# Transfers spaced by matmul work, and the fourth expert pass sent home by scatters: a macaron layer with experts

## The chip, the cores and the metric

The kernel runs on one core of one Trainium2 chip. The metric is the device time of one execution in microseconds (us), lower is better; the value quoted is the median of three runs. The core's engines are TensorE (PE, with its weight loads PEld), VectorE (DVE), ScalarE (ACT), GpSimd (POOL) and SyncE (SP). POOL issues the indirect DMAs, SP the plain ones.

## The reference

Eight sequences of 512 tokens with 128 features (D) pass through a feed-forward layer with experts, an attention, and the same feed-forward layer again, each on a layernorm of its input with a residual. All in float32.

```python
x = x + 0.5 * ffn(layernorm(x))
x = x + attn(layernorm(x))
x = x + 0.5 * ffn(layernorm(x))

def ffn(x):          # 8 experts, each token goes to its best 2
    logits = x @ router_w + router_b
    scores, idx = top_k(logits, 2); gates = softmax(scores)
    for each expert e:   # c_e: the token's gate for e, or 0
        out += (relu(x @ W1[e] + b1[e]) @ W2[e] + b2[e]) * c_e    # 128 -> 512 -> 128

def attn(x):         # 16 heads of 8, causal, over each sequence
    q, k, v = x @ w_qkv;  q, k rotated in half of the heads
    p = softmax(q k^T / sqrt(8) + decay bias, causal)
    return (p v) @ w_o
```

## The kernel before

**Six expert passes.** Only the two experts of each token are computed. For this the tokens are sorted by expert: each normalised token row is scattered twice into a "room" in DRAM (`xs`), which has a fixed number of rows for each expert (351 or 480). An expert pass then runs over the eight experts of a room: it fetches an expert's rows by a plain DMA (`xb`, L933), transposes them (`turn`, L976), multiplies by W1 in pieces of 128 hidden features (`wide`, L989, with the relu on ACT, L996), and by W2 in tiles of up to 120 rows (`out`, L1013, with the bias on DVE, L1017, into `ysb`). The first feed-forward layer has the passes f0 (sequences 0 and 1, 351 rows), f1 (2, 3, 4; 480) and f2 (5, 6, 7; 480), the second g0, g1 and g2 over the same sequences.

**Routing.** `route` does for one sequence: layernorm (statistics L758 and L761, variance L763 on DVE, `rstd` on POOL by a power, recorded at L474, `xn` L769 on DVE), transposes on PE (L784) and their copy on DVE (L786), router logits (L814, L818), ranks and places (L827 to L870, `posb` at L857, `to` at L866), and eight scatters of 128 rows on POOL (L875). The attention of a sequence has a layernorm of the same form (`rstd_a`, `xn_a`).

**Two ways back to the tokens.** f0, f1, f2 and g0 are untagged: SP writes an expert's results to DRAM (`ys`, 175.5 or 240 KB) by one plain DMA (L1024), and POOL later gathers them by token, eight gathers of 128 rows a sequence (`combine`, recorded at L474), each pair followed by two DVE additions with the gates (L1073). g1 and g2 are tagged: a token row carries its home address in two more columns; `homes` (three small DVE operations an expert, L943 to L951) turns it into row numbers, POOL scatters each result tile to its token's place (`send`, L957), and `collect` (L1110) reads a sequence back by plain loads into `yr` and adds on DVE (L1114).

**The order.** The work is laid out in units: a lead (units -30 to -1: f0 and most of f1's start), a core (0 to 95: eight sequences, four head groups and three steps each, of the attention, with the rest of f1, then f2, g0 and the start of g1 between them) and a tail (96 to 126: g1's rest and g2). `surround` emits one unit: a quota of pieces of the running expert pass, the unit's attention work, and the due steps of other streams (`at`, `routed`, `combined`, each given a unit). PE, ACT, DVE and SP follow an order written by hand from that; on POOL `in_turn` keeps the program's order. Indirect DMAs are queued as jobs (scatters and gathers) or results (sends), and `transfer()` records the next one:

```python
    def transfer(self, second=False):

        if self.jobs and (
            not second or any(urgent for urgent, _ in self.jobs)
            or (len(self.jobs) > 4 and not self.results)
        ):
            self.jobs.popleft()[1]()
        elif self.results:
            self.results.popleft()()
```

A unit calls it after the first causal mask, at its end, and in the tail also once between. Each recorded transfer waits for the evacuation of a matmul result that was the newest when it was recorded (its "mark", `behind_mark`). Spare DMAs on SP clear the rooms ahead of their use; those of rooms 3 and 4 wait in `later`, one for each unit from unit 12 on.

Of the kernel before, what the change touches and what calls it, by code (L numbers as in the profile page):

```python
# [11 lines left out]
FP = mybir.dt.float32  # L12
# [8 lines left out]
P = 128  # L21
B, N, D = 8, 512, 128
T = N // P
# [22 lines left out]

ROOMS = [(2, 351, False), (3, 480, False), (3, 480, False), (3, 480, True), (3, 480, True)]
CAP = max(cap for _, cap, _ in ROOMS)  # L50
NOWHERE = 1e6
CT = -(-CAP // P)
STOP = object()

# [394 lines left out]
class Group:  # L449


    def __init__(self, seqs, cap, key, xs, ys, tagged):
        self.seqs, self.cap, self.key, self.xs, self.ys = seqs, cap, key, xs, ys
        self.tagged, self.width = tagged, D + 2 * tagged
        self.ct = -(-cap // P)
        self.rows = cap // self.ct
        assert self.ct * self.rows == cap
        self.parts = [(t, min(3 if cap > 4 * P else 4, self.ct - t))
                      for t in range(0, self.ct, 3 if cap > 4 * P else 4)]
        self.placed = 0  # L460
        self.pieces = E * (len(self.parts) * (1 + C) + self.ct) + 1


# [19 lines left out]
class Main:  # L483
    def __init__(self, tc, ctx, aps):
# [15 lines left out]


        self.jobs, self.results, self.mark = deque(), deque(), None
        self.adds, self.unit = deque(), 0
        const = self.const

# [48 lines left out]
            partial(nc.sync.dma_start, self.wo_sb, aps["w_o"]),  # L554
        ])
        self.loads.extend(partial(self.clear, 2, t) for t in range(4))
        self.later = deque(partial(self.clear, i, t) for i in (3, 4) for t in range(4))
        self.later.extend(partial(self.clear_results, i) for i in (3, 4))


        self.ident = ident = const.tile([P, P], FP, name="ident")
# [88 lines left out]
# [6 lines that stand above are left out]
            self.jobs.popleft()[1]()  # L656
        elif self.results:
            self.results.popleft()()

    def additions(self):  # L660

# [262 lines left out]
    def experts(self, g):  # L924
# [31 lines left out]
        def send(e, t, ys):  # L956
            ins = nc.gpsimd.indirect_dma_start(  # L957
                out=g.ys[:, :],
                out_offset=bass.IndirectOffsetOnAxis(ap=home[e][:rows, t : t + 1], axis=0),
                in_=ys[:rows, t, :], in_offset=None,  # L960
            ).ins
            tc.declare_no_dep(ins, group=f"ys_{key}", reason="no two rows have the same home")
            tc.add_to_no_dep_group(f"ys_{key}", ins)
            self.in_turn(ins, scatter=True)
            self.behind_mark(ins)

        def up(e, xb):

            xT = self.fp.tile([P, CAP], FP, tag="xT", name=f"xT_{key}_{e}")
            h = self.fp.tile([P, C, CAP], FP, tag="h", name=f"h_{key}_{e}")  # L970

            def turn(t0, nt):
                n0, n = t0 * rows, nt * rows
                tp = self.bank([P, N], f"xbT_ps_{key}_{e}_{t0}")
                for t in range(nt):
                    nc.tensor.transpose(  # L976
                        tp[:, ts(t, rows)], xb[:rows, t0 + t, :D], self.ident[:rows, :rows]
                    )
                if self.evac == "act":
                    nc.scalar.copy(xT[:, n0 : n0 + n], tp[:, :n])  # L980
                else:
                    nc.vector.tensor_copy(xT[:, n0 : n0 + n], tp[:, :n])
                if g.tagged and t0 == 0:
                    homes(e, xb)

            def wide(t0, nt, c):
                n0, n = t0 * rows, nt * rows
                z = self.bank([P, N], f"z_{key}_{e}_{n0}_{c}")
                nc.tensor.matmul(  # L989
                    z[:, :n], self.w1_sb[:, e, ts(c, P)], xT[:, n0 : n0 + n],  # L990
                    start=True, stop=True,
                )
                bias = self.b1T[:, e * C + c : e * C + c + 1]
                dst = h[:, c, n0 : n0 + n]
                if self.evac == "act":
                    ins = nc.scalar.activation(dst, z[:, :n], AF.Relu, bias=bias)  # L996
                else:
                    ins = nc.vector.tensor_scalar(dst, z[:, :n], bias, 0.0, ALU.add, ALU.max)  # L998
                self.mark = ins.ins

            return (
                h, [partial(turn, *p) for p in g.parts],
                [partial(wide, *p, c) for p in g.parts for c in range(C)],
            )

        def down(e, h):

            ys = self.fp.tile([P, CT, D], FP, tag="ysb", bufs=5, name=f"ysb_{key}_{e}")

            def out(t):  # L1010
                y = self.bank([P, D], f"y_{key}_{e}_{t}")
                for c in range(C):
                    nc.tensor.matmul(  # L1013
                        y[:rows], h[:, c, ts(t, rows)], self.w2_sb[:, e, c, :],
                        start=(c == 0), stop=(c == C - 1),
                    )
                ins = nc.vector.tensor_tensor(  # L1017
                    ys[:rows, t, :], y[:rows], self.b2_sb[:rows, e], ALU.add
                )
                self.mark = ins.ins  # L1020
                if g.tagged:
                    self.results.append(partial(send, e, t, ys))
                elif t == g.ct - 1:
                    nc.sync.dma_start(  # L1024
                        g.ys[: E * g.cap, :].rearrange("(t p e) d -> e p t d", p=rows, e=E)[e],
                        ys[:rows, : g.ct],
                    )

            return [partial(out, t) for t in range(g.ct)]
# [69 lines left out]
    def collect(self, g, i, dst, parts=1):  # L1099

        nc = self.nc
        b = g.seqs[i]
        x = self.x[b]
        if i % 2 == 0:
            self.pair = self.p2.tile([P, 2, T, 2, D], FP, tag="ee", name=f"yr_{b}")
        yr = self.pair[:, i % 2]
        src = g.ys[2 * N * i : 2 * N * (i + 1), :].rearrange("(t p r) d -> p t r d", p=P, r=2)
        n = T // parts
        for k in range(parts):
            nc.sync.dma_start(yr[:, ts(k, n)], src[:, ts(k, n)])  # L1110
        yield
        for t in range(T):
            for r in range(2):
                nc.vector.scalar_tensor_tensor(  # L1114
                    x[:, t, :], yr[:, t, r], g.gates[:, i, t, r : r + 1], x[:, t, :],
                    ALU.mult, ALU.add,
                )
            if t % n == n - 1:
                k = t // n
                nc.sync.dma_start(  # L1120
                    dst[b].rearrange("(t p) d -> p t d", p=P)[:, ts(k, n)], x[:, ts(k, n)]
                )
            if parts == 1:
                yield
# [179 lines left out]
def macaron_kernel(  # L1304
# [24 lines left out]
    def run(*streams):  # L1329
        for s in streams:  # L1330
            for _ in s:
                pass
# [23 lines left out]
    with ExitStack() as main:  # L1356
# [5 lines left out]
        f0 = m.open_group([0, 1], 351, 0, "f0")  # L1362
        f1 = m.open_group([2, 3, 4], 480, 1, "f1")
        f2 = m.open_group([5, 6, 7], 480, 2, "f2")
        g0 = m.open_group([0, 1], 351, 1, "g0")
        g1 = m.open_group([2, 3, 4], 480, 3, "g1")
        g2 = m.open_group([5, 6, 7], 480, 4, "g2")
        order = [f0, f1, f2, g0, g1, g2]
# [55 lines left out]
        ]  # L1424
        fills = {}

        def surround(n, att):

            m.unit = n
# [21 lines left out]
                    m.oT = (*m.held[:2], got)  # L1451
            m.held = (*units[n], ee) if att else None
            m.evac = "dve" if att and n % seq not in (8, 9, 10) else "act"
            run(take(fill, 1 if quota else 0))
            m.evac = "act"
            if att:
                m.causal(units[n][2], ee, 0)
            m.transfer()
            if last is not None:
                m.outputs(*last)  # L1460
            if att:
# [5 lines left out]
            for k, (stream, steps) in enumerate(work):  # L1467
                some = todo // (len(work) - k + 1)
                run(take(stream, steps))
                run(take(fill, some))  # L1470
                todo -= some
            if n >= core and len(m.jobs) + len(m.results) > 2:
                run(take(fill, todo // 2))
                todo -= todo // 2
                m.transfer(second=True)
            run(take(fill, todo))
            m.additions()
            m.transfer(second=True)

        m.held = m.oT = None  # L1480
        with m.banks(("m", 8)):
# [22 lines left out]
            for b in range(B):  # L1504
                u = b * seq
                if b == 2:
                    combined(7, f1, 0, urgent=True, ahead=True)
                elif b > 2:
                    combined(u - (17 if b == 5 else 21), *place[True][b], urgent=b == 5, ahead=b == 5)
                if b > 0:  # L1510
                    at(u - 10, m.project(b), 8)
                for g in range(G):
# [1 line left out]
                at(u + seq + 2, m.finish(b), 2, 2 if b == B - 1 else 1)  # L1514
                routed(u + seq + (3 if b == B - 1 else 4), *place[False][b], urgent=b in (1, 4, 5, 6, 7), ahead=b in (4, 6, 7))
            for i in range(2):
                combined(79 + 7 * i, g0, i, out)
            for i in range(3):
                at(tail + 2 + 3 * i, m.collect(g1, i, out), 5)
            at(tail, m.verdict(bad), 2)  # L1520
# [76 lines left out]
```

## Time and profile before

| | before |
|---|---|
| three runs, us | 700.78, 701.87, 702.69 |
| median, us | 701.87 |
| the profiled execution, us | 700.09 |
| its span, us | 698.3 |
| mean granted PE clock | 0.977 |
| PE busy | 629.2 us, 90% |
| DVE busy | 410.2 us, 59% |
| ACT busy | 341.3 us, 49% |
| POOL busy | 300.3 us, 43%, 322 instructions |
| scatters into rooms, L875 | first layer 40 at 974 ns and 24 at 989 ns, second layer 64 at 998 ns |
| gathers, recorded at L474 | first layer 64 at 1013 ns, second layer 16 at 1053 ns |
| sends, L957 | 64, 996 ns each |

A profile is one execution; its span runs from the first to the last instruction, and the execution's own time is 1.8 us longer. Rows of a timeline give the start, the duration, engine, line and operation, then output and inputs by the names in the program without their numbers, and in brackets how long the engine stood idle before and what released it. `xn_f` is thus the `xn` of any sequence of the first layer, `xn_g` of the second, `xn_a` of the attention. In the clock row of the slices a 9 is full speed.

### The profile page before, as it was taken

The page shows a single profiled execution, that of the slowest core. Times are in us where ns is not written, and L with a number is a line of the kernel's source. Part 1 is how long each engine was busy: PE and PEld are TensorE (multiplying, and loading weights), DVE is VectorE, ACT ScalarE, POOL GpSimd, SP SyncE. Part 2 cuts the span into 40 slices and gives each one's busy share as a digit, 9 for nine tenths or more (in the row PEclk, how much of TensorE's full clock was granted, in tenths as well). Part 3 has the DMA queues.
Part 4 walks back from the last instruction along what each step waited for, and adds up shares of the span by engine and source line. Part 5 has one row for each costly group of instructions (what it writes and reads, how often), then busy time and mean ns, then how long its engine had stood idle before and what let it go on. Part 6 is the DMA issues. An engine that isn't in the chain of part 4 may idle for free. (4 is left out here: it accounts for less than half of the span.)

```text
span 698.3 us, 13045 instructions
## 1 busy us (share of the span) xinstructions
PE 629.2 (90%) x4867; PEld 410.3 (59%) x4867; DVE 410.2 (59%) x1442; ACT 341.3 (49%) x548; POOL 300.3 (43%) x322
## 2 busy tenths in 40 slices
PE   3269999999999999999999999999999998969980
PEld 2148867756465656556656656656456656747760
DVE  6736448734466666675687677676666654433414
ACT  4034443455755656565665565555665552234420
POOL 3744637642223223314154423424144556575660
PEclk9999999999999999999999999999999999889995
DMA  8747843312409921111211111101402111145324
GB/s 265 197 136 209 205 115 98 85 45 77 101 22 172 264 69 38 30 29 43 71 32 49 40 38 38 30 27 39 105 27 75 35 31 42 53 121 140 104 58 143
DMA packets 78670, 61.06 MB, mean 87 GB/s; under 512 B 7392, under 2 KB 70792, under 8 KB 78600
## 3 DMA queue, kind: packets, MB, share of 16 engines
q1 hardware_dynamic: 69608, 42.51, 23.8%
q0 software_dynamic: 8704, 17.63, 8.5%
q8 instruction: 41, 0.67, 0.4%
q14 instruction: 29, 0.24, 0.1%
q10 hardware_dynamic: 288, 0.01, 0.0%
HBM read 26.34 MB, written 33.78 MB: 86 GB/s over the span
## 5 line engine op out<-in xcount | busy, mean ns | idle before, releaser
L1208 ACT ACTIVATE ee<-st 128x768 f32<-128x768 f32 (+1 forms) x192 | 159.0, 881 | 104.1 <-PE st L1201 100.6
L474 POOL DMA_INDIRECT yt_f<-ys,back_f x64 | 64.8, 1013 | 133.5 <-DVE ee L1215 55.7
L1215 DVE TENSOR_TENSOR ee<-ee,keep 128x256 f32<-128x256 f32 (+1 forms) x192 | 93.5, 507 | 25.4 <-ACT ee L1208 25.3
L1013 PEld LDWEIGHTS y_g<-w_sb,h_g 128*120 128x120 f32 (+1 forms) x704 | 87.1, 184 | 27.4 <-issue 21.7
L875 POOL DMA_INDIRECT xs<-xn_g,to_g x64 | 63.8, 998 | 90.1 <-DVE ee L1215 34.9
L1013 PEld LDWEIGHTS y_f<-w_sb,h_f 128*120 128x120 f32 (+1 forms) x704 | 85.9, 182 | 28.5 <-issue 16.2
L1201 PE MATMUL st<-qT,kT 32*128 32x512 f32 (+3 forms) x1024 | 96.1, 467 | 2.3 <-ACT h_f L996 0.8
L1013 PE MATMUL y_f<-w_sb,h_f 128*120 128x128 f32 (+1 forms) x704 | 93.9, 277 | 0.2 <-DVE h_f L998 0.2
L989 PE MATMUL z_g<-xT_g,w_sb 128*128 128x480 f32 (+1 forms) x192 | 92.6, 569 | 1.3 <-ACT xT_g L980 1.3
L1013 PE MATMUL y_g<-w_sb,h_g 128*120 128x128 f32 (+1 forms) x704 | 93.0, 277 | 0.6 <-DVE o_tok L1250 0.3
L1227 PE MATMUL o<-ee,vpad 128*32 128x512 f32 (+3 forms) x1024 | 89.4, 442 | 0.8 <-DVE ee L1215 0.8
L989 PE MATMUL z_f<-xT_f,w_sb 128*128 128x480 f32 (+1 forms) x192 | 88.8, 551 | 1.0 <-ACT xT_f L980 1.0
L996 ACT ACTIVATE h_f<-z_f,b1T 128x480 f32<-128x480 f32 (+1 forms) x86 | 53.5, 623 | 68.2 <-PE z_f L989 67.3
L957 POOL DMA_INDIRECT ys<-ysb_g,home_g x64 | 63.7, 996 | 39.3 <-ACT h_g L996 8.7
L1017 DVE TENSOR_TENSOR ysb_f<-y_f,b_sb 120x128 f32<-120x128 f32 (+1 forms) x88 | 25.0, 287 | 77.9 <-PE y_f L1013 74.2
L996 ACT ACTIVATE h_g<-z_g,b1T 128x480 f32<-128x480 f32 (+1 forms) x71 | 45.7, 646 | 47.4 <-PE z_g L989 46.7
L1201 PEld LDWEIGHTS st<-qT,kT 32*128 32x128 f32 x1024 | 43.1, 183 | 32.6 <-issue 8.1
L1017 DVE TENSOR_TENSOR ysb_g<-y_g,b_sb 120x128 f32<-120x128 f32 (+1 forms) x88 | 25.1, 287 | 58.2 <-PE y_g L1013 57.6
L1227 PEld LDWEIGHTS o<-ee,vpad 128*32 128x32 f32 x1024 | 23.5, 108 | 52.4 <-issue 7.5
L875 POOL DMA_INDIRECT xs<-xn_n,to_f x40 | 39.0, 974 | 34.9 <-ACT xi_sb L727 8.1
L989 PEld LDWEIGHTS z_g<-xT_g,w_sb 128*128 128x128 f32 x192 | 30.1, 195 | 26.6 <-issue 15.2
L989 PEld LDWEIGHTS z_f<-xT_f,w_sb 128*128 128x128 f32 x192 | 30.2, 194 | 13.8 <-issue 7.2
(186 smaller groups left out, 778.7 us busy)
## 6 DMA issues: line engine op xcount, KB each, us to landing
w_sb<-in_L_ffn_W_dram SPq DMA_DIRECT2D x16, 256.0 KB
xs<-zeros SPq DMA_DIRECT2D x8, 487.5 KB
xb_g<-xs SPq DMA_DIRECT2D x16, 243.8 KB
xb_f<-xs SPq DMA_DIRECT2D x16, 240.0 KB
ys<-ysb_f SPq DMA_DIRECT2D x16, 240.0 KB
ys<-zeros SPq DMA_DIRECT2D x2, 1536.0 KB
x<-in_L_attn_x_dram SPq DMA_DIRECT2D x8, 256.0 KB
xs<-zeros SPq DMA_DIRECT2D x1, 1920.0 KB
```

The source lines that it names most:

```text
L474: ins = op(*args, **kw)
L875: ins = nc.gpsimd.indirect_dma_start(out=g.xs[:, :], out_offset=bass.IndirectOffsetOnAxis(ap=g.to[:, i, t, r : r + 1], axis=0), in_=xn[:, ...
L957: ins = nc.gpsimd.indirect_dma_start(out=g.ys[:, :], out_offset=bass.IndirectOffsetOnAxis(ap=home[e][:rows, t : t + 1], axis=0), in_=ys[:r ...
L989: nc.tensor.matmul(z[:, :n], self.w1_sb[:, e, ts(c, P)], xT[:, n0 : n0 + n], start=True, stop=True,)
L996: ins = nc.scalar.activation(dst, z[:, :n], AF.Relu, bias=bias)
L1013: nc.tensor.matmul(y[:rows], h[:, c, ts(t, rows)], self.w2_sb[:, e, c, :], start=(c == 0), stop=(c == C - 1),)
L1017: ins = nc.vector.tensor_tensor(ys[:rows, t, :], y[:rows], self.b2_sb[:rows, e], ALU.add)
L1201: nc.tensor.matmul(st[:, h, c0 : c0 + N - kt * P], kT[r0 : r0 + SLOT, ts(kt, P)], qT[r0 : r0 + SLOT, kt * P :], start=True, stop=True,)
L1208: nc.scalar.activation(ee[:, two, :width], st[:, two, :width], AF.Exp)
L1215: ins = self.nc.vector.tensor_tensor(d, d, self.keep.unsqueeze(1).unsqueeze(1).to_broadcast([P, 2, len(parts), P]), ALU.min,)
L1227: self.nc.tensor.matmul(self.o[h * SLOT : (h + 1) * SLOT, kt * P :], self.vpads[b % 2][:, kt, 4 * g + h, :], ee[:, h, c0 : c0 + n], start= ...
```

## The change

There are two parts. First, g0 becomes a tagged pass with a room of its own (a sixth, with one more set of clears): its 24 result tiles are scattered by `send`, and `collect` reads its two sequences back in the core, at units 82 and 88. The 16 gathers of g0 and its 8 plain result writes are gone. The gathers of four sequences are entered two units earlier, and those of sequences 6 and 7 as urgent. `ysb` has four buffers for five.

Second, outside the core a unit no longer has fixed places for transfers. `work` counts the columns that PE has been given (transposed rows, the width of each wide product, 512 for a result tile, and 350 for each step of another stream); after each piece a transfer is recorded if the count is at 830 or over, and each transfer takes 830 off. In the core a unit has its two places as before.

```diff
-ROOMS = [(2, 351, False), (3, 480, False), (3, 480, False), (3, 480, True), (3, 480, True)]
+ROOMS = [(2, 351, False), (3, 480, False), (3, 480, False), (3, 480, True), (3, 480, True), (2, 351, True)]
+SPACING = 830
...
-        self.later = deque(partial(self.clear, i, t) for i in (3, 4) for t in range(4))
-        self.later.extend(partial(self.clear_results, i) for i in (3, 4))
+        self.later = deque()
+        for i, parts in ((5, 3), (3, 4), (4, 4)):
+            self.later.extend(partial(self.clear, i, t) for t in range(parts))
+            self.later.append(partial(self.clear_results, i))
...
         elif self.results:
             self.results.popleft()()
+        self.work = max(self.work - SPACING, 0)
...
+                self.work += nt * rows          # turn
...
+                self.work += n                  # wide
...
-            ys = self.fp.tile([P, CT, D], FP, tag="ysb", bufs=5, name=f"ysb_{key}_{e}")
+            ys = self.fp.tile([P, CT, D], FP, tag="ysb", bufs=4, name=f"ysb_{key}_{e}")
...
+                self.work += C * D              # out
...
-        if i % 2 == 0:
+        if self.unit < 96:
+            self.pair = self.p1.tile([P, 1, T, 2, D], FP, tag="yr", name=f"yr_{b}")
+        elif i % 2 == 0:
             self.pair = self.p2.tile([P, 2, T, 2, D], FP, tag="ee", name=f"yr_{b}")
-        yr = self.pair[:, i % 2]
+        yr = self.pair[:, i % self.pair.shape[1]]
...
-        g0 = m.open_group([0, 1], 351, 1, "g0")
+        g0 = m.open_group([0, 1], 351, 5, "g0")
...
+        def pieces(fill, n, att):
+
+            for _ in take(fill, n):
+                if not att and m.work >= SPACING:
+                    m.transfer()
+                yield
...
-            run(take(fill, 1 if quota else 0))
+            run(pieces(fill, 1 if quota else 0, att))
             m.evac = "act"
             if att:
                 m.causal(units[n][2], ee, 0)
-            m.transfer()
+                m.transfer()
...
-                run(take(fill, some))
+                run(pieces(fill, some, att))
                 todo -= some
-            if n >= core and len(m.jobs) + len(m.results) > 2:
-                run(take(fill, todo // 2))
-                todo -= todo // 2
+                if not att:
+                    m.work += 350
+            run(pieces(fill, todo, att))
+            m.additions()
+            if att:
                 m.transfer(second=True)
-            run(take(fill, todo))
-            m.additions()
-            m.transfer(second=True)
...
-                    combined(u - (17 if b == 5 else 21), *place[True][b], urgent=b == 5, ahead=b == 5)
+                    combined(u - (17 if b == 5 else 23), *place[True][b], urgent=b > 4, ahead=b == 5)
...
-                combined(79 + 7 * i, g0, i, out)
+                at(82 + 6 * i, m.collect(g0, i, out), 5)
```

More of the change, by code (lines that the diff above doesn't have):

```diff
@@ L459, in __init__ @@
                       for t in range(0, self.ct, 3 if cap > 4 * P else 4)]
-        self.placed = 0
+        self.placed = self.sent = 0
         self.pieces = E * (len(self.parts) * (1 + C) + self.ct) + 1
@@ L502, in __init__ @@
         self.jobs, self.results, self.mark = deque(), deque(), None
+        self.work = 0
         self.adds, self.unit = deque(), 0
@@ L965, in send @@
             self.behind_mark(ins)
+            g.sent += 1
         def up(e, xb):
@@ L1103, in collect @@
         x = self.x[b]
-        if i % 2 == 0:
+        if self.unit < 96:
+            self.pair = self.p1.tile([P, 1, T, 2, D], FP, tag="yr", name=f"yr_{b}")
+        elif i % 2 == 0:
             self.pair = self.p2.tile([P, 2, T, 2, D], FP, tag="ee", name=f"yr_{b}")
-        yr = self.pair[:, i % 2]
+        yr = self.pair[:, i % self.pair.shape[1]]
+        assert g.sent == E * g.ct
         src = g.ys[2 * N * i : 2 * N * (i + 1), :].rearrange("(t p r) d -> p t r d", p=P, r=2)
```

## The prediction

> **What bounds the kernel now.** The page's first two sections come first: engine shares, then slices.
>
> ```profile
> span 698.3 us, 13045 instructions
> PE 629.2 (90%) x4867; PEld 410.3 (59%) x4867; DVE 410.2 (59%) x1442; ACT 341.3 (49%) x548; POOL 300.3 (43%) x322
> PE   3269999999999999999999999999999998969980
> PEclk9999999999999999999999999999999999889995
> ```
>
> PE is 90% busy, and every slice from the fifth (70 us) to the 33rd is full. Time can be won or lost only where PE waits: in the first 45 us, which the change leaves alone, and between 580 and 620 us. What is now hidden beside a full PE can only become a loss. The windows of that stretch (columns: length, PE, PEld, DVE, ACT, POOL busy, clock, DMA share, GB/s) and PE's timeline there say what it waits for.
>
> ```profile
> 580.00:600.00 20.00, 17.25 (x93) 13.26 (x92) 9.52 (x41) 4.34 (x7) 11.97 (x12) 0.83 0.13 39
> 600.00:620.00 20.00, 14.68 (x89) 11.08 (x88) 6.53 (x29) 4.54 (x8) 13.72 (x15) 0.88 0.44 113
> ...
> 589.66 1.26 PE L784 MATMUL xnT_ps_g<-ident,xn_g 128*128 128x128 f32 x4 [1.87 <-DVE xn_g L769]
> 591.71 1.88 PE L814 MATMUL lg_ps_g<-rw_sb,xnT_g 128*128 128x8 f32 x8 [0.78 <-DVE xnT_g L786]
> ...
> 616.69 1.03 PE L976 MATMUL xbT_ps_g<-ident,xb_g 120*128 120x120 f32 x4 [4.67 <-DMA xb_g<-xs]
> ```
>
> The last sequence's layernorm (1.87 us) opens a chain, router, 8 scatters, fetch, whose end PE waits 4.67 us for. From 616.69 us on PE is full to 677 us, so a microsecond won in the chain is won at the end. POOL's timeline at its head, and in the lead, where two layernorms pass through the same queue:
>
> ```profile
> 587.15 1.00 POOL L474 DMA_INDIRECT yt_g<-ys,back_g  x1 [0.31 <-issue]
> 588.16 1.06 POOL L474 TENSOR_TENSOR rstd_g<-var_g,neg_half 128x4 f32<-128x4 f32 x1
> ...
> 82.15 0.96 POOL L875 DMA_INDIRECT xs<-xn_n,to_f  x1 [0.30 <-issue]
> 83.41 0.96 POOL L875 DMA_INDIRECT xs<-xn_n,to_f  x1 [0.30 <-issue]
> ...
> 78.28 1.07 POOL L474 TENSOR_TENSOR rstd_f<-var_f,neg_half 128x4 f32<-128x4 f32 x1
> 116.33 1.04 POOL L474 TENSOR_TENSOR rstd_f<-var_f,neg_half 128x4 f32<-128x4 f32 x1
> 117.36 1.00 POOL L474 TENSOR_TENSOR rstd_a<-var_a,neg_half 128x4 f32<-128x4 f32 x1
> ```
>
> A transfer holds POOL for 0.97 us and the next starts 0.30 us later: one per 1.27 us (82.15 to 83.41). An rstd stands in the same queue in program order, behind every transfer recorded before it; PE's transposes L784 stand behind that.
>
> **The change, part by part.** The instruction orders of both programs give PE and ACT unchanged; DVE, POOL and SP differ.
>
> *Tail.* All gathers of g0 are gone from POOL, the one at 587.15 among them. rstd then follows the send that ends at 586.85: 586.87 for 588.16, a gain of 1.3 us in the chain. Two additions L1073 (0.73 us at 598.05), which stood ahead of posb L857, go too. What is next depends on the clock. PE's clock is 0.5 from 591.24 to 598.06 us, two stretches of 3.41 us, and logits, transposes, a wide pair and eight second products take 1.88, 1.04, 1.82 and 1.92 us there for 0.96, 0.58, 0.97 and 1.04 elsewhere: 3.1 us more. With the idle 1.87 cut to about 0.6 that fall may not come. Gain: 1.3 us if it does; if not, posb moves from 598.69 to about 594.8, the scatters' first from 600.92 to 597.0, and the gain is 3.9. The wait of 4.67 us stays, since PE's work before it moves too. One scatter gap of 1.40 us among the eight may go (1.1 us more), so the ends are 1.3 and 5.0; I take 3.0, nearer to the fall staying out, because the idle is cut by two thirds.
>
> *Lead.* Spacing lets a transfer out for each 830 columns of PE work. In f1's pass PE takes 1.68 us (103.56 to 105.24) for two wide products and one result tile, 960 + 512 columns, so 830 columns are 0.95 us, less than the 1.27 us slot. POOL then runs without pause, and more transfers than before stand ahead of each rstd. By slots and before's evacuation times:
> - Before rstd of sequence 5 now stand all 16 scatters of sequences 3 and 4. They start at 61.40 (mark 61.13): 61.40 + 16 x 1.27 - 0.30 = 81.42, so rstd ends at 82.49 (79.35 before). PE's L784 began at 81.19; xn takes 1.2 us of DVE and the last transpose follows 0.4 later: end 84.12 for 81.79, a stall of 2.3. The fetch of f1, for which PE waited 0.84 us at 90.58, no longer waits for these scatters: -0.8. Net 1.5.
> - Gathers of f0 start at 94.72 (96.2 with that shift). Eight gathers and two scatters precede rstd of sequence 6: 96.2 + 10 x 1.27 - 0.3 + 1.07 = 109.7 (105.69). xn, L784 end at 111.2; before 108.3, with the shift 109.8. Stall 1.4, sum 2.9.
> - Ten more slots precede the rstds of sequence 7 and of attention 0: 109.7 + 0.19 + 12.4 = 122.3, ends 123.4 and 124.4 (117.37, 118.36). Attention's L784 then ends at 125.95; before 120.46, shifted 123.4. Stall 2.6, sum 5.5.
> - DVE keeps its order, and in the new one four additions of sequence 1 stand ahead of the copies L786 of sequence 7 (120.51 before). The last one's gather ends at 125.35 + 1.5 = 126.85. From a gather's end to its data no row of the lead is bound; a scatter's end at 87.03 released a fetch at 88.38, and the last send's end at 681.55 landed at 683.35: 1.35 to 1.8, I take 1.6. Additions and copies then give L814 its input at 130.1, where it would have begun at 128.35. Stall 1.9, sum 7.4.
> - The additions that ended at 135.83 ahead of qpad L1165 are gone, and with them PE's wait of 0.88: 6.5 us.
>
> Lower bound: if POOL's transfers come back inside the slots as PE's own lateness spreads, the last two stalls go: 1.5 + 1.4 - 0.9 = 2.0. Upper bound: each stall could halve the clock as the one at 587.80 did, 3.1 us a time: 6.5 + 6.2 for two.
>
> A rule and this row part here. In the trace PE's clock fell at 591.24 after a stretch of 3.41 us (from 587.83) with 2.2 us of idle and sparse transposes in the rest. The Trainium skill (TensorE: Matmul & The Clock Gate, Part 1 and its table of advice) has the clock halve after an idle window of about 3.4 us that runs freely, and advises against idle gaps over about 3 us; by that no lead stall costs more than its length, and by the row each may. The page adds that transposes do not count as busy in the same way, which would join the two, and 6.83 us is two of its windows. I take the middle: no fall in the likeliest case, one in the next.
>
> *Core.* 24 home operations on DVE (L943, 947, 951: 0.16, 0.17, 0.16 us at 596.11), eight trios of 0.5 us. PE's L1227 waited 0.8 us in all for DVE over 1024 matmuls, so they lie under cover; uncovered they cost 8 x 0.5 = 4.0. 24 sends for 16 gathers are 8 x 1.27 = 10 us of POOL, which is 43% busy; the order leaves each attention rstd where it stood. The plain loads of g0: one of g1 was issued at 633.06 and used at 639.06, 6.0 us; g0's first goes out at about 499.5 and is used after 514. Removed additions and added ones are both 16. Clears of 2.5 MB more ride in slices that moved 172 and 264 GB/s: some 10 us of DMA time, and f1's additions have 5.6 us of slack. Bounds -1 to +4, taken +0.5: the nearest row, PE's 0.8 us, says covered. Fewer buffers for results (4 for 5) cost nothing while a result leaves within four experts, some 50 us in the core; without that cover an expert waits one 1.27 us slot.
>
> **Sum.** +6.5 +0.5 -3.0 = +4.0. The profiled execution took 700.09 us around its span of 698.3, so 704.1; the median of the runs is 701.87, 1.8 more than that execution, so 705.9 us. A measurement here can tell 0.3%, about 2.1 us, from no change.
>
> **Rivals.**
> - *Faster.* POOL's train breaks up and only the first lead stalls are paid (+2.0), while the clock's fall in the tail stays out and the odd gap goes (-5.0), core 0: -3.0, 698.9 us. For it: the tail is worth its gain undiluted. Against: the slots of 1.27 us at 16.92 to 25.45 us show that POOL does not go faster, and the marks of the third train have passed up to 6 us before its slots come (109.95 for 116.00). It decides at the third rstd: started before about 119 us, this side wins.
> - *Nothing to measure.* +3.5 in the lead, as the third stall overlaps the fourth, +0.5, -4.0: 701.9.
> - *Slower still.* One lead stall fills a clock stretch, or two: 705.9 + 3.1 = 709.0, or 712.1. For it the row at 591.24; against it that lead stalls are interleaved with matmuls that are dense.
> - *The change does not space.* If 830 columns seldom bind, transfers leave as before in number: lead 0, tail -3.0, 698.9. The new order speaks against it: rstd stands behind more transfers, not fewer. It is part of the faster side's chance.
>
> **How the numbers follow.** The sum as worked out, 0.45; slower still, 0.17; nothing to measure, 0.20; faster, 0.18. The range reaches from the faster case's figure, 698.9, to 711.5, which leaves out the end of the two-fall case. The likeliest case's own range is 703.6 to 707.8 (tail 5.0 to 1.3, landing 1.35 to 1.8). Faster 0.18, same 0.20, slower 0.62.
>
> **What would show it.** rstd in the lead at 81.4, 108 to 109 and 122 to 124 us, ending right behind unpaused transfers, and PE's L784 waiting for xn by 1 to 3 us each. PE's attention starting 5 to 7 us later than at 136.81. In the tail, rstd right behind a send, L814 at 0.96 us instead of 1.88, and the wait for the fetch still near 4.7 us. Wrong, if the lead's L784 show no wait, if the clock row shows 0.5 in the lead, or if PE waits in the core for DVE.

## The result and the profile after

The changed kernel takes 706.43 us (median; 704.91 to 707.51), the kernel before 701.87: a ratio of 1.0066, interval 1.0052 to 1.0080, 4.6 us slower. The profiled execution took 707.51 us around its span of 705.4, the longest of its runs, while that of before (700.09) lies below all of its own, so the two traces differ by 7.1 us, more than the medians do. Of the seven runs after, the two fastest (704.91, 704.97) are the two with a granted PE clock of 0.98; the other five, the profiled one among them, have 0.975 to 0.977. Line numbers have moved: L784 is now L789, L875 is L880, L957 is L962, L976 is L982, L1073 is L1082.

Engine shares and slices of the profile after:

```profile
span 705.4 us, 13078 instructions
PE 633.4 (90%) x4867; PEld 412.1 (58%) x4867; DVE 413.6 (59%) x1470; ACT 341.8 (48%) x548; POOL 309.0 (44%) x331
PE   3269999899999999999999999999999998979970
PEclk9999999999999999999999999999999999889995
```

PE has the same 4867 instructions and one slice below 9 in what was its unbroken stretch. PE's timeline after (start, duration, and in brackets the wait and its releaser), in the lead and then in the tail:

```profile
83.34 1.01 PE L789 MATMUL xnT_ps_f<-ident,xn_f 128*128 128x128 f32 x4 [1.64 <-DVE xn_f L774]
111.31 1.25 PE L789 MATMUL xnT_ps_f<-ident,xn_f 128*128 128x128 f32 x4 [1.37 <-DVE xn_f L774]
125.40 1.10 PE L789 MATMUL xnT_ps_f<-ident,xn_f 128*128 128x128 f32 x4 [2.11 <-DVE xn_f L774]
...
596.88 1.09 PE L789 MATMUL xnT_ps_g<-ident,xn_g 128*128 128x128 f32 x4 [0.84 <-DVE xn_g L774]
598.76 1.88 PE L819 MATMUL lg_ps_g<-rw_sb,xnT_g 128*128 128x8 f32 x8 [0.78 <-DVE xnT_g L791]
622.59 1.03 PE L982 MATMUL xbT_ps_g<-ident,xb_g 120*128 120x120 f32 x4 [3.37 <-DMA xb_g<-xs]
```

Three waits for `xn` that were not there now stand in the lead. In the tail the two waits are shorter (0.84 for 1.87, 3.37 for 4.67). The logits still take 1.88 us, so PE was again at half clock. POOL's timeline shows what `xn` waits for:

```profile
79.50 0.96 POOL L880 DMA_INDIRECT xs<-xn_n,to_f  x1 [0.30 <-issue]
80.77 0.96 POOL L880 DMA_INDIRECT xs<-xn_n,to_f  x1 [0.30 <-issue]
81.75 1.06 POOL L475 TENSOR_TENSOR rstd_f<-var_f,neg_half 128x4 f32<-128x4 f32 x1
...
122.86 1.04 POOL L475 DMA_INDIRECT yt_f<-ys,back_f  x1 [0.30 <-issue]
123.92 1.05 POOL L475 TENSOR_TENSOR rstd_f<-var_f,neg_half 128x4 f32<-128x4 f32 x1
124.95 1.00 POOL L475 TENSOR_TENSOR rstd_a<-var_a,neg_half 128x4 f32<-128x4 f32 x1
```

Transfers stand back to back, 1.27 us apart, and rstd follows right behind the last of them. It starts at 81.75, 109.79, 123.92 and 124.95 us where before had 78.28, 104.64, 116.33 and 117.36.

Since PE runs the same instructions in the same order, each can be set against itself. PE stands 0.34 us behind before at 45.8 us, 2.5 after the first L789, 4.6 after the second, 6.9 to 7.3 after the third, 8.8 from 131.0 us on, 7.8 at qT (L1190, 144.57), 8.2 from 351.8 us on, 7.2 at the last layernorm, 5.9 at the fetch (622.59) and 6.6 from 629 on.

### The profile page after: what moved, and what is told of

Its sections match the earlier page's. It is cut to its first block, busy times and chain, and to the rows that moved or that the text cites. A ratio compares the mean times of both kernels' runs of the same rounds, so it can differ in the third digit from the quotient of the medians.

```text
span 705.4 us, 13078 instructions
## 1 busy us (share of the span) xinstructions
PE 633.4 (90%) x4867; PEld 412.1 (58%) x4867; DVE 413.6 (59%) x1470; ACT 341.8 (48%) x548; POOL 309.0 (44%) x331
## 5 line engine op out<-in xcount | busy, mean ns | idle before, releaser
L962 POOL DMA_INDIRECT ys<-ysb_g,home_g x88 | 88.6, 1007 | 88.9 <-DVE ysb_g L1025 21.1
L880 POOL DMA_INDIRECT xs<-xn_g,to_g x64 | 63.7, 995 | 92.9 <-DVE ee L1227 24.6
L1025 DVE TENSOR_TENSOR ysb_f<-y_f,b_sb 120x128 f32<-120x128 f32 (+1 forms) x88 | 25.0, 288 | 75.5 <-PE y_f L1021 71.9
L1025 DVE TENSOR_TENSOR ysb_g<-y_g,b_sb 120x128 f32<-120x128 f32 (+1 forms) x88 | 25.1, 288 | 62.5 <-PE y_g L1021 61.7
L880 POOL DMA_INDIRECT xs<-xn_n,to_f x40 | 38.9, 974 | 30.5 <-ACT h_f L1003 12.5
```

The source lines that it names most:

```text
L880: ins = nc.gpsimd.indirect_dma_start(out=g.xs[:, :], out_offset=bass.IndirectOffsetOnAxis(ap=g.to[:, i, t, r : r + 1], axis=0), in_=xn[:, ...
L962: ins = nc.gpsimd.indirect_dma_start(out=g.ys[:, :], out_offset=bass.IndirectOffsetOnAxis(ap=home[e][:rows, t : t + 1], axis=0), in_=ys[:r ...
L1025: ins = nc.vector.tensor_tensor(ys[:rows, t, :], y[:rows], self.b2_sb[:rows, e], ALU.add)
```

## The experiments

Ratios are to the kernel before on the same chip, with 95% intervals; a difference in us behind a ratio is worked out from the ratio, unless medians are named.

**Where the price lies.** The queue theory says that the lead's transfers ahead of rstd cost everything and the tail gains. The rival says that g0's new way home costs it. `m.spaced` switches the spacing on for some units only.

`lead_old`: the fixed places back in the lead alone.

```diff
-                if not att and m.work >= SPACING:
+                if m.spaced and m.work >= SPACING:      # m.spaced = n >= core
...
+            if not m.spaced:
+                m.transfer()                            # and second=True, as before
```

> The changed kernel with the lead's two fixed places for transfers put back; the tail stays spaced and g0 stays tagged. Queue theory (the lead's loss is rstd waiting in POOL's queue): rstd of sequences 5, 6, 7 and of attention 0 at 78.3, 104.6, 116.3 and 117.4 us as before, no wait at L789 in the lead, PE level with before until 580 us; the tail keeps its 2.3 us; about 699.6 us. Rival (the price lies in g0's scatters, homes, loads and clears in the core): 704 to 706 us, with PE falling behind between 140 and 580 us.

Measured 700.36 us against 702.66 for before on that chip, ratio 0.9966 (0.9951 to 0.9982): 2.4 us faster. No wait at L789 is left in the lead, and PE does not fall behind between 140 and 340 us. The 3.3 us that it is behind before at 134 us come from its start (0.9) and from the f1 fetch (1.24 us of wait for 0.84, and one stretch of half clock behind it, 94.44 to 97.86), not from a layernorm.

`lead_only`: the same switch as `m.spaced = n < 0`, with g0 untagged and before's units for the gathers.

> The kernel before with the spacing in the lead alone; g0 untagged, core and tail with their fixed places. Queue theory: the whole lead loss, rstd at 81.4, 108 to 111, 121 to 126 us, PE about 8 us late at 140 us, no gain in the tail: about 709.5 us. Rival (price in g0's way home): 702 us, as before.

Measured 710.54 us, ratio 1.0123 (1.0102 to 1.0144): 8.6 us slower than before (7.9 by the medians), against the rival's zero. Its waits on PE (in total, times, longest) are those of the changed kernel:

```profile
PE xnT_ps_f L789 <- DVE xn_f L774: 5.1, 3, 2.1
```

`tag_only`: `m.spaced = False`, g0 tagged.

> The changed kernel with fixed places for transfers everywhere, so that g0's scatters and plain loads (with their clears and the earlier gathers) stand alone. Queue theory: lead as before; in the tail the gather ahead of rstd and two additions ahead of posb are gone, 1.0 to 2.3 us: about 700.2 us. Rival (price in g0's way home): 704 to 706 us.

Measured 702.0 us, ratio 0.9985 (0.9971 to 0.9998): 1.1 us faster (0.7 by the medians), at or below the low end of the 1.0 to 2.3 us that were expected. With fixed places a send has taken the gather's place ahead of the last rstd: PE's wait there is 1.85 us, as before. Only the scatters' start came earlier, 12.9 us after the last variance for 14.9. So the 1.0 us by which that wait is shorter in the changed kernel belongs to the tail's spacing and not to the gather's removal alone.

**Is it rstd's place, or the spacing as such?** `hold` keeps everything and records no transfer in the units of the lead's layernorms.

```diff
+HOLD = (-22, -21, -14, -13, -10, -9)
...
-                if not att and m.work >= SPACING:
+                if not att and m.work >= SPACING and m.unit not in HOLD:
```

> The changed kernel, with one addition: in six units of the lead (the two in which each of the three layernorms there is computed) no transfer is recorded, so that POOL has drained when rstd comes; the spacing is the same otherwise. Queue theory: rstd at 78.0, 104.6, 116.3 and 117.4 us, no waits at L789 in the lead, the old waits of 0.84 us (fetch of f1) and 0.88 us (qpad) smaller, tail gain 2.3 us: about 698.5 us. Rival (spacing costs by crowding the DMA queues or DVE, wherever rstd stands): PE still 4 to 8 us late at 140 us, about 705 us.

Measured 699.28 us, ratio 0.9954 (0.9937 to 0.9971). One line takes the lead's whole loss away: PE stands 0.5 to 1.5 us behind before up to 140 us, 1.1 of it from before the first layernorm. rstd waits for its variance again, not for the queue:

```profile
105.66 1.04 POOL L476 TENSOR_TENSOR rstd_f<-var_f,neg_half 128x4 f32<-128x4 f32 x1 [3.87 <-DVE var_f L769]
117.58 1.05 POOL L476 TENSOR_TENSOR rstd_f<-var_f,neg_half 128x4 f32<-128x4 f32 x1 [3.09 <-DVE var_f L769]
```

The f1 fetch (0.81 us) and qpad (1.02) still wait, which the expectation had put lower. `hold_again`, on a third chip:

> The kernel hold once more, as the base for the three beside it: about 0.995 of the kernel before. Rival (its lead over before belongs to one chip): 1.00 or above.

699.48 against 702.78 us, ratio 0.9947 (0.9926 to 0.9968).

**The size of the spacing, and the clock, on a chip apart.** Four kernels ran on a second chip, where the kernel before takes 715.71 us.

`lead_1000` takes 1000 columns for 830 where the unit is below 0.

> The changed kernel with 1000 columns for 830 in the lead alone. Queue theory, by slots of 1.27 us and the marks of before: rstd of sequences 5, 6, 7 and attention 0 at 78.9, 104.9, 117.5 and 118.6 us, at most 1.2 us later than before, so waits at L789 of 1 us or less in all; about 700 us. Rival (spacing by matmul work costs whatever its size, by crowding DMA queues or DVE): PE 4 to 8 us late at 140 us, about 705 us.

Ratio 1.0084 (1.0055 to 1.0113). The time is inconclusive: PE waits there 4.12 us at L1214 for an `h_f` (from 154.56) and 3.34 us at L850 (from 141.13); in the traces from the other chips these two products wait 0.75 us at most. The three kernels below ran on the same chip with the lead of `hold`, and they wait at the same two products, 3.3 to 4.4 us and 1.7 us. So these waits go with the chip and not with the 1000 columns; what makes them stays open. Neither the changed kernel nor `hold` ran on that chip. Its trace does bear on the queue: L790 waits 0.9 us in all in the lead, for 5.1 at 830 columns, though PE's own lateness there gives POOL some of that time.

The other three add matmuls that nothing reads, to `hold`; `warm_all`, and `warm_all2` further on, also record no transfer in unit 100, between the last rstd and the last scatters:

```diff
+    def warm(self, n, key):
+        z = self.bank([P, N], f"warm_{key}")
+        for _ in range(n):
+            self.nc.tensor.matmul(
+                z[:, :480], self.ident, self.w1_sb[:, 0, :480], start=True, stop=True)
...
+        if key == "g2_7": self.warm(2, "a")       # ahead of the transposes, and "b" ahead of the logits
...
+        if key == "g2": self.warm(7, "c")         # in experts, ahead of the first transposes
```

> The kernel hold, and seven matmuls of 480 columns whose result nothing reads, on PE just ahead of the wait for the last room's first fetch (0.41 us each, 2.9 of the 3.27 us). Clock theory: the half clock that follows this wait (613.76 to 620.59 us in hold, 5.9 us of it with PE at work) stays out, 2.9 us less than hold: about 696.4 us. Rival (the clock falls there for another reason than PE's idle time, or the fetch is what counts): 699.3 us.

> The kernel hold, and twice two such matmuls around the transposes of the last layernorm, where PE waits 0.83 and 0.78 us. The half clock of 593.28 to 596.69 us should stay out. Queue theory: six sends stand in POOL's queue between rstd and the first scatter and end at 599.37, so the scatters cannot start over 0.2 us earlier: about 699.1 us. Rival (PE's clock sets the chain): posb 1.6 us earlier and with it the end, about 697.6 us.

> The kernel hold with both sets of matmuls, and with no transfer recorded in the unit between the last rstd and the last scatters, so that three sends go behind the scatters. Queue and clock theory together: first scatter at about 597.3 for 599.83 us, 2.2 us won ahead of the fetch, and 2.9 us behind it: about 694.2 us. Rival (each set is hidden): 699.3 us.

In this order, the ratios are 1.0087 (1.0054 to 1.0120), 1.0093 (1.0058 to 1.0127) and 1.0165 (1.0129 to 1.0201). The size of the sets was wrong by two. PE's timeline of `warm_fetch`:

```profile
638.83 5.80 PE L677 MATMUL warm_c<-w_sb,ident 128*128 128x480 f32 x14
```

Seven products are 14 matmul records: a float32 product of 480 columns is two records of 0.41 us each. The set lasted 5.8 us and not 2.9, and outlasted the wait it stood in. So these times say nothing on what the clock is worth. The clock itself did what was expected in two of the three: no half clock behind the fetch in `warm_fetch`, none at the layernorm in `warm_ln`. In `warm_all` there was none at the layernorm, but the clock fell at 635.94 us, as its set ahead of the fetch began. And all four kernels with spacing are slower than before on this chip, where `hold` is faster than before on two others. No trace of before was taken here, so whether the gain of `hold` holds on this chip is open.

**The clock, at the right size.** One product for two at the layernorm, three for seven at the fetch, beside `hold_again`:

> The kernel hold with three matmuls (480 columns in float32, 0.81 us each as two passes) for seven ahead of the wait for the last room's first fetch, 2.4 us of the 3.3. Clock theory: no half clock behind the wait, PE starts on the last room no later, 2.9 us less than hold_again. Rival (the wait of the fetch sets the end and the clock behind it is hidden): the same as hold_again.

697.33 us, ratio 0.9909 (0.9886 to 0.9932), 2.2 us below hold_again by the medians. PE needs 58.6 us from its start on the last room to its end, for 61.2: 2.6 us, close to the 2.9 of the clock theory. But it starts there 28.2 us after the last variance and not 26.7 as in hold_again, where the layernorm's half clock was one stretch and not two; "no later" had been expected. The two traces thus differ by 1.2 us at PE's end, the medians by 2.2.

> The kernel hold with one such matmul (0.81 us) ahead of the last layernorm's transposes and one ahead of its logits, where PE waits 0.83 and 0.78 us. No half clock there. Queue theory: the sends between rstd and the scatters still hold POOL, so 0.2 us less than hold_again. Rival (PE's clock sets the chain): 1.6 us less.

698.58 us, ratio 0.9933 (0.9909 to 0.9957). The first scatter stands 11.65 us after the variance for 11.87, so the sends do hold POOL. PE gets the fetch 0.3 us earlier; the medians differ by 0.9, which the intervals do not tell from 0.3.

> The kernel hold with both smaller sets of matmuls and three of the six sends behind the last scatters. Queue and clock theory together: the first scatter 2.2 us earlier, no half clock in the tail, 2.2 + 2.9 = 5.1 us less than hold_again, about 694 us where before takes 702.5. Rival (each is hidden behind the other): 0 to 2 us less.

696.16 us, ratio 0.9901 (0.9877 to 0.9924), the best of all, 3.3 us below hold_again by the medians (5.1 were expected) and 6.6 below before. The clock is whole through the tail (windows: length, PE, PEld, DVE, ACT, POOL busy, clock, DMA share, GB/s):

```profile
580.00:600.00 20.00, 18.71 (x116) 13.35 (x115) 11.48 (x54) 6.28 (x12) 10.81 (x12) 1.00 0.11 33
600.00:620.00 20.00, 18.60 (x102) 12.72 (x101) 7.21 (x24) 6.75 (x11) 15.43 (x16) 1.00 0.44 112
```

The 2.2 us ahead of the fetch were not: the first scatter came at 11.10 us for 11.87, 0.8 us. One send still stood ahead of the scatters and ended at 598.68, and the first scatter then started 0.98 us later, released by DVE:

```profile
597.69 0.99 POOL L974 DMA_INDIRECT ys<-ysb_g,home_g  x1 [2.93 <-DVE posb_g L874]
599.66 1.00 POOL L892 DMA_INDIRECT xs<-xn_g,to_g  x1 [0.98 <-DVE ex_g L924]
```

## Why the prediction was right, and where its terms were off

The forecast was +4.0 us, and +4.6 was measured, by the mechanism named: saturated POOL in the lead, rstd behind it, less a gain in the tail. `lead_only` and `hold` show the first part with the change made alone and taken away alone, `lead_old` the second. The terms in order:

- **The rate of the transfers.** The reading behind it failed. "x2" at L989 is one wide product of 480 columns in two records, not two products. So 1.68 us are 480 + 512 columns, and 830 columns are 1.40 us of matmul work, slower than the 1.27 us slot. The conclusion held, since `work` also counts the transposes and 350 for each step. Before's marks for the 16 scatters of sequences 3 and 4 run from 61.13 to 75.78, one per 0.98 us. About 3,800 of the 12,450 columns for that stretch must come from these two terms; that is worked out, not tried. The same misreading doubled the first `warm` sets.
- **The three rstds**: predicted ends 82.49, 109.7, 123.4 and 124.4; measured 82.81, 110.88, 124.97 and 125.95. Slot counting from one row was enough.
- **The stalls at L789**: 2.3, 1.4 and 2.6 predicted; the shifts there are 2.15, 2.1 and 2.3 to 2.7.
- **The fetch of f1**: -0.8 was predicted, -0.1 came (0.72 us of wait left). The term failed because the scatters were not the last thing that the fetch waits for: on SP it stands behind the last of three result writes (at 90.00 us), which waited for its own evacuation (L1025, until 89.97).

```profile
77.44 12.86 SPq L1033 DMA_DIRECT2D ys<-ysb_f  x3
90.42 1.23 SPq L938 DMA_DIRECT2D xb_f<-xs  x2
```

- **The additions ahead of the copies**: 1.9 predicted (its own times, 130.1 and 128.35, make 1.75), 1.5 seen, but not as a wait. DVE did wait for the gathers (1.5 to 1.6 us from a gather's end to its data; 1.6 was taken):

```profile
128.66 0.41 DVE L1082 SCALAR_TENSOR_TENSOR x<-yt_f,gates_f,x 128x128 f32<-128x128 f32 x1 [0.66 <-DMA yt_f<-ys,back_f]
130.04 0.35 DVE L1082 SCALAR_TENSOR_TENSOR x<-yt_f,gates_f,x 128x128 f32<-128x128 f32 x1 [0.97 <-DMA yt_f<-ys,back_f]
130.64 0.68 DVE L791 COPY xnT_f<-xnT_ps_f 128x512 f32<-128x512 f32 x1
```

  PE ran at half clock from 127.56 to 130.97 and its products filled just that time, so the two costs overlap and the trace cannot say which is worth how much of the 1.5.
- **qpad**: -0.88 predicted, -1.0 came. The lead as a whole: 6.5 predicted, 7.4 in the trace (0.34 of its 7.76 us stood there before the lead's work). From `hold` to the changed kernel the ratios differ by 1.1 to 1.2%, some 8 us.
- **The core**: +0.5 predicted, +0.46 in the trace, at one place. Three home operations stand on DVE ahead of `o_tok`, for which PE waits at L1151 (0.68 us for 0.22), in every kernel with g0 tagged and not in `lead_only`. The cover was not complete: a trio's 0.5 us is paid once in eight. The loads of g0 went out at 507.75 and 542.17 and nothing waited.
- **The tail**: 3.0 predicted, 1.6 in PE's trace, 2.4 net of the core by `lead_old`'s runs. rstd gave 1.0 (1.3) and the odd scatter gap went (eight scatters in 9.84 us for 11.00). The bet that the clock would not fall with the idle time cut by two thirds was lost, and by the fetch's end the half clock took 0.7 us more of PE's work than before, since PE began closer to the stretch's start.

The faster rival fell at its own point: the third rstd started at 123.9, not before 119. The slower rival's clock fall did come once in the lead, where DVE's wait stood beside it. The lead's loss was taken too small (6.5 for some 8) and so was the gain of tail and core together (2.5, where `hold` lies 3.4 us below before), and the two errors nearly cancel: the path was read rightly, and that the sum came within 0.6 us of the measured change is in part luck.

Of the signs set down beforehand, the starts of rstd came within 0.8 us and the waits at the lead's transposes as told. The last logits did not run at full clock (1.88 us again), the wait for the fetch fell to 3.37 us instead of staying at 4.7, and PE's attention began 7.8 us later, not 5 to 7. Two of the three signs of being wrong also came, both small: half clock in the lead, one stretch of 3.41 us, and a wait of PE for DVE in the core, 0.46 us.

## What to carry to other kernels

An instruction of a microsecond that a chain waits for must not share an in-order queue with traffic that is only kept short on average: count the transfers recorded ahead of it, times the slot, and if that passes the time of its input, leave a pause there. Spacing by work done is worth its gain only with that pause (`hold` against the changed kernel, 8 us for one line, on two chips; on the slower chip the gain is not shown). And when a wait on PE is cut, look at the clock behind it: three products that nobody reads, sized to the wait, were worth 2.2 us by the medians, where the spacing in the tail was worth 1.6 (`lead_old` against `tag_only`).

## What was not expected of the hardware

PE's clock fell in the tail after a stretch of 3.41 us (595.19 to 598.60) with only 0.84 + 0.62 us of idle time, the rest products and transposes. In the lead a stretch with 1.25 us of a wait and eight transposes (124.15 to 127.56) did the same, and waits of 1.64 and 1.37 us elsewhere did not. The rule cited in the prediction (the Trainium skill, TensorE: Matmul & The Clock Gate, Part 1: an idle window of about 3.4 us) would have spared both stretches; the measurement decides, and the row of before was the better guide. Idle time alone does not sort such stretches, counted in steps of 3.41 us from a trace's falls: in `lead_old` the clock fell after one (592.79 to 596.20) with 0.78 us of idle time, and in the changed kernel it stayed up after one (110.49 to 113.91) with 0.9 us. Counting transposes as idle does not sort them either: `lead_old` kept its clock after 0.73 us of idle time and some 2 us of transposes (497.21 to 500.63), 2.7 us together, where the tail stretch above has 2.6. What counts is not shown. A product of 0.81 us on each side of the transposes kept the clock up (`warm_ln1`, no half clock there), and without the fall behind the fetch PE's work there was 2.6 us shorter (`warm_fetch3` against `hold_again`).
